# Five moves of work in a gated attention and expert layer: head sums, block turning, query copies, a shared multiply, and pool order

## The chip, the cores and the metric

The kernel runs on one core of a Trainium2 chip. The metric is the time of the whole program on the device in microseconds (us); the time before is the median of three runs. The engines of the core are named as in the profile: PE (matrix engine), DVE (vector engine), ACT (scalar engine), POOL (GpSimd) and SP (the engine that here issues most of the DMA transfers). Each takes its own instructions strictly in order, and waits for the others by semaphores.

## The reference

A layer with gates: cross attention to a short context, then a mixture of experts, both added to the input through a tanh gate.

```python
# x (4, 512, 512), ctx_512 (4, 64, 128), float32; 16 heads of 32; 8 experts, top 2, inner width 256
def attn(q, latent_kv, Wq, Wkv_expand, Wout):
    k, v = split(latent_kv @ Wkv_expand.T)           # 64 keys a batch
    scores = einsum('bhqd,bhkd->bhqk', heads(q @ Wq.T), heads(k)) / sqrt(32)
    scores = where(tril(ones((512, 64))), scores, finfo.min)
    return merge(softmax(scores) @ heads(v)) @ Wout.T

def ffn(x, gate_w, w1, w2, w3, ws1, ws2, ws3):
    weights, idx = top_k(softmax(x @ gate_w.T), 2)
    y = sum over the two chosen e of weights * (silu(x @ w1[e].T) * (x @ w3[e].T)) @ w2[e].T
    z = silu(x @ ws1.T) * (x @ ws3.T) @ ws2.T        # the shared expert
    return y + z

x = x + tanh(g_xattn[0]) * attn(layernorm(x), ctx_512, Wq, Wkv_expand, Wout)
x = x + tanh(g_ffn[0]) * ffn(layernorm(x), ...)
```

## The kernel before

**Stages.** Attention runs from 0 to 184 us, once for each batch `b` of 512 tokens (four tiles `t` of 128 tokens). `last_routing` (184 to about 230 us) finishes the last batch: its output projection, second layernorm, gate, and the scatter of rows to their experts, with the shared expert in between. Then 34 expert tiles of 128 rows follow (to 430 us), which fetch rows by expert, multiply by w1 and w3 (L947), by w2 (L974), and add into `y_d`. A tail joins the two experts of each token, the shared expert and the residual.

**Order.** Attention and `last_routing` are under a manual schedule of all five engines: the order of the instructions on each engine is the order in which the Python code issues them. A step of batch `b` carries pieces of three batches: the scores and softmax of `b`, the output projection and second layernorm of `b - 1` (called `last`), and the first layernorm, transposes and query projection of `b + 1` and `b + 2`.

**The step of one batch**, in the order of issue in `attention()`: the products of scores for tiles 0 and 1 (`score_products`, into `psc`, the one buffer of pool `ps_s`); `largest` (the mask is added for tile 0, L321, then the maximum, L322) and `exponentials` (difference on DVE, L327, exponential on ACT, L328) of tiles 0 and 1, which gives p0 and p1; then the output projection of `last` by tiles (`project_out`: PE L368 into `pd`, DVE adds to `xs`, L372) with `moments` of the result; the turning of blocks for `b + 1`; `deviation` (a square root on ACT, L162, then `table_of(AF.Exp)`, a second table load, L675); the second half of the scores; the query projection of `b + 1` by quarters (`project_q`: PE L290 into `pq`, ACT copies to `qt`, L294); p2 and p3; `transpose_p` of p0 and p1 (PE L343 into `pp`, ACT copies to `prt`, L346); and so on. `ps_mm`, which `pd`, `pq`, `pp`, `pt` and others share, has four buffers.

**How the rows of the first layernorm are transposed.** For b = 0 and 1, PE transposes them (`turn`, L195, copies on ACT, L196). For b = 2 and 3, `first_rows` calls `passed` (L501 to L512): DVE normalizes the rows, SP writes them to DRAM (`xn_d`, four transfers of 256 KB) and reads them back with blocks in other places (`xg`, four transfers of 256 KB, in pieces of 128 floats, each filling 32 partitions of `xg`). Then `turn_blocks` (L517, four stream transposes of 32x32 blocks on DVE) makes `xt`. `first_rows(2, ...)` is issued at the end of the step of b = 0, so its `turn_blocks` stands in the step of b = 1; that of b = 3 stands in the step of b = 2.

**The start.** `head_of` (L118) holds, by partition, which of two heads the partition belongs to: two reductions of the identity matrix on DVE. The keys `kt` are made from the product `pk` by two scaled copies on ACT (L689) and two on DVE (L696), both scaled with `head_of`.

**The end of routing.** `fill(n)` draws n matmuls of the shared expert from `shared_in_turn`; when it draws the last one of a pair, the silu on ACT (L640) and a multiply on DVE (L641) are issued. `fill_ends` computes the ends of the experts' regions and issues eight transfers of zeros, half on SP and half on ACT. `tile_table` (L580 to L617) is a chain of DVE operations that makes a table of the tiles: first row, expert and rank of each. SP reads `row_of`, PE reads `expert_of`.

**Memory pools of attention.** `aw`, `ab`, `a2` and `a4` are allocated in this order and released together; then `w13_all`, the experts' first weights, is laid over their place.

Of the kernel before, what the change touches and what calls it, by code (L numbers as in the profile page):

```python
# [13 lines left out]
F32 = mybir.dt.float32  # L14
# [5 lines left out]
P = 128  # L20
# [28 lines left out]
def gated_cross_attention_moe(  # L49
# [64 lines left out]
    nc.gpsimd.memset(taken[0], 0.0)  # L114

    head_of = const.tile([P, 2], F32, name="head_of")
    for j in range(2):
        nc.vector.tensor_reduce(  # L118
            head_of[:, j : j + 1],
            ident.rearrange("p (i j d) -> p j i d", i=2, j=2)[:, j, :, :], AX.XY, ALU.add,  # L120
        )

    mask = const.tile([P, 1, 1, SK], F32, name="mask")
    nc.gpsimd.memset(mask, 0.0)
# [85 lines left out]
    weights = ctx.enter_context(ExitStack())  # L210

    with ExitStack() as attn:
        aw = attn.enter_context(tc.tile_pool(name="aw", bufs=1))
        ab = attn.enter_context(tc.tile_pool(name="ab", bufs=1))
        a2 = attn.enter_context(tc.tile_pool(name="a2", bufs=2))
        a4 = attn.enter_context(tc.tile_pool(name="a4", bufs=4))

        scoring = attn.enter_context(ExitStack())
        ps_s = scoring.enter_context(tc.tile_pool(name="ps_s", bufs=1, space=PSUM))


        wkv_sb = aw.tile([L, 2 * D], F32, name="wkv_sb")
        wo_sb = al.tile([P, DC, D], F32, name="wo_sb")
        ctx_sb = aw.tile([L, B, 2, SK], F32, name="ctx_sb")
        for t in range(2):
            nc.sync.dma_start(out=xs[0][:, t, :], in_=x[ts(t, P), :])
        nc.sync.dma_start(out=ctx_sb[:, :, 0, :], in_=ctx_t)
# [46 lines left out]
        def project_values(b):  # L274

            pv = ps_mm.tile([P, NPAIR, 2, HD], F32, tag="mm", name="pv")
            nc.tensor.matmul(
                pv.rearrange("p n j d -> p (n j d)"),
                ctx_sb[:, b, :, :].rearrange("p r k -> p (r k)"),
                wkv_sb[:, D : 2 * D], start=True, stop=True,  # L280
            )
            for j in range(2):
                r = slice(j * SK, (j + 1) * SK)
                nc.scalar.copy(vals[r, b, :, :], pv[r, :, j, :])
# [40 lines left out]
        def exponentials(pr, by_row, src, mx):  # L325

            nc.vector.tensor_tensor(by_row, src, mx, ALU.subtract)  # L327
            nc.scalar.activation(pr, pr, AF.Exp, scale=1.0 / math.sqrt(HD))  # L328
            return pr
# [147 lines left out]
            return places, scatter  # L477

        def new_xt():
            return ab.tile([P, DC, S], F32, tag="xt", name="xt")  # L480

        def new_qt():
            return a2.tile([P, DC, S], F32, tag="qt", name="qt")
# [11 lines left out]
            return passed(xn, b) if b > 1 else xn  # L495

        def new_xn():
            xn = ab.tile([P, QT, D], F32, tag="xn", name="xn")
            return [xn[:, t, :] for t in range(QT)]

        def passed(xn, b):  # L501


            for t in range(QT):
                nc.sync.dma_start(out=xn_d[b][ts(t, P), :], in_=xn[t])
            xg = ab.tile([P, QT, QT, P], F32, tag="xn", name="xg")
            for a in range(DC):
                nc.sync.dma_start(
                    out=xg[ts(a, HD)].rearrange("k t tb n -> k (t tb) n"),
                    in_=xn_d[b][:, ts(a, P)].rearrange("(t k) n -> k t n", k=HD),  # L510
                )
            return xg  # L512

        def turn_blocks(xg, dst):

            for t in range(QT):
                nc.vector.transpose(  # L517
                    dst[:, :, ts(t, P)].rearrange("p c (tb k) -> p tb c k", k=HD),
                    xg[:, t].rearrange("p tb (c i) -> p tb c i", c=DC),
                )  # L520
# [147 lines left out]
        def attention():  # L668
# [4 lines left out]
            def table_of(function):  # L673

                nc.scalar.activation(small_one, ones[:, 0:1], function)  # L675


            pw = ps_mm.tile([P, P], F32, tag="mm", name="pw")
            for _ in range(10):
# [37 lines left out]
            for b in range(B):  # L717
                more, last = b + 1 < B, b - 1
                prt = ab.tile([P, NPAIR, S], F32, tag="prt", name="prt")
                psc = score_products(b, 0, qt)  # L720
                if b > 1:
                    places, scatter = route(last - 1, *chosen)
                if more:
                    xt, qt_next = new_xt(), new_qt()
                    if not b:
                        turn(xn, xt)
                if not b:
                    project_values(1)
                p0 = exponentials(*largest(psc, 0))
                p1 = exponentials(*largest(psc, 1))  # L730
                if not b:
                    nc.scalar.activation(tg_x, tg_x, AF.Tanh)
                    nc.scalar.activation(tg_f, tg_f, AF.Tanh)
                if b > 1:
                    places()
                softmax(p0)
                if b:
                    mv, rstd = new_stats()
                    project_out(last, at, 0)
                    moments(last, mv, 0)  # L740
                softmax(p1)
                if b > 1:
                    for t in range(QT):
                        scatter(t)
                if b:
                    for t in range(1, QT):
                        project_out(last, at, t)
                        moments(last, mv, t)
                        if more and t == 1:
                            turn_blocks(xn, xt)  # L750
                    rest = deviation(mv, rstd)
                    if more:
                        table_of(AF.Exp)
                else:
                    project_q(xt, qt_next, range(2))
                    first_rest = first_moments(b + 2)
                    table_of(AF.Exp)
                psc = score_products(b, 1, qt)
                if not b:
                    transpose_p(p0, prt, 0)  # L760
                    transpose_p(p1, prt, 1)
                if b and more:
                    project_q(xt, qt_next, range(1))
                elif b:
                    gated, _ = shared_pair(*next(parts))
                    table_of(AF.Exp)
                p2 = largest(psc, 2)
                if b:
                    rest()
                p2 = exponentials(*p2)  # L770
                p3 = largest(psc, 3)
                if more:
                    p3 = exponentials(*p3)
                if b:
                    if more:
                        project_q(xt, qt_next, range(1, 2))
                    else:
                        gated()
                    xn2 = new_rows(last)
                    second_rows_of(xn2, last, mv, rstd)  # L780
                softmax(p2)
                if more:
                    softmax(p3)
                if b:
                    transpose_p(p0, prt, 0)
                    transpose_p(p1, prt, 1)
                    if not more:
                        turn(xn2, x2t[last])
                if more:
                    project_q(xt, qt_next, range(2, 3))  # L790
                    if b:
                        turn(xn2, x2t[last])
                    if b + 2 < B:
                        if b:
                            first_rest = first_moments(b + 2)
                            table_of(AF.Exp)
                        xn = first_rows(b + 2, first_rest)
                    project_q(xt, qt_next, range(3, DC))
                    if b == B - 2:
                        load_shared()  # L800
                    if b:
                        scored = gate(last)
                else:
                    p3 = exponentials(*p3)
                    softmax(p3)
                    gated, scored = shared_pair(*next(parts), lambda: gate(last))
                    gated()
                    scores = by_token(scored)
                transpose_p(p2, prt, 2)
                if not b:  # L810
                    project_values(2)
                elif more:
                    scores = by_token(scored)
                transpose_p(p3, prt, 3)
                if not b:
                    project_values(3)
                attended = []

                def attend_now():
                    attended.append(attend(b, prt))  # L820

                if b:
                    chosen = (xn2, *choose(last, scores, attend_now))
                else:
                    attend_now()
                (at,) = attended
                qt = qt_next
# [7 lines left out]
        def last_routing(at, chosen, parts):  # L835
# [3 lines left out]
            def fill(n):  # L839
                for _ in range(n):  # L840
                    next(filling)
# [31 lines left out]
            fill_ends(n)  # L873
            for t in range(QT):
                scatter(t)
            table = tile_table(n)
            for _ in filling:
                pass
# [274 lines left out]
```

## Time and profile before

| what | value |
|---|---|
| median of the runs before | 465.02 us (464.71 to 465.4) |
| the profiled execution | 463.8 us |
| its span, first instruction to last | 462.1 us |
| mean granted clock of PE | 0.998 |
| PE busy | 445.0 us of the span |
| DVE busy | 257.3 us |
| POOL busy | 178.5 us |
| ACT busy | 125.1 us |
| longest wait of PE behind a copy of queries (b = 2) | 2.07 us |
| idle of DVE ahead of the mask add of b = 1 | 4.29 us |
| idle of ACT ahead of its first copy of keys | 2.25 us |

The busy time of an engine says how much work it has over the whole span; it does not say which engine sets the end of a stage. For that one reads, in the timeline, what an engine was idle for: the bracket behind an instruction gives the idle time just before it and the instruction that ended it. The profiled execution was 1.2 us shorter than the median of the runs, and the span leaves out another 1.7 us around the program.

### The profile page before, as it was taken

How to read it: one execution, taken by the hardware profiler on the slowest of the kernel's cores; microseconds unless marked ns; L12 is line 12 of the kernel's file. 1: busy time of each engine (PE TensorE's matmuls, PEld its weight loads, DVE VectorE, ACT ScalarE, POOL GpSimd, SP SyncE). 2: the span in 40 equal slices, each digit the busy share in tenths (PEclk: the TensorE clock that was granted, in tenths of full speed). 3: DMA queues.
4: the chain of work that ended last, by engine and by line, in shares of the span. 5: the costliest groups of instructions: out<-in, count | busy, mean ns of one | idle time of the engine just before them, and what ended most of it. 6: DMA issues, size and time to landing. Idle time of an engine off the chain costs nothing.

```text
span 462.1 us, 6310 instructions
## 1 busy us (share of the span) xinstructions
PE 445.0 (96%) x1754; PEld 228.0 (49%) x1754; DVE 257.3 (56%) x613; ACT 125.1 (27%) x237; POOL 178.5 (39%) x184
## 2 busy tenths in 40 slices
PE   6999999899899999999999999999999999999994
PEld 6875545564455554454444444444444444444342
DVE  5759699789928974548223333334433333432385
ACT  3357613652354275322101111111111111111000
POOL 2003312303840573332400656555655655565400
PEclk9999999999999999999999999999999999999999
DMA  8987250070403040999943877666656666544598
GB/s 270 315 292 279 91 92 0 1 177 6 176 22 84 23 165 1 357 417 417 403 110 84 166 125 123 107 97 100 93 93 102 103 103 97 78 48 51 78 383 315
DMA packets 60800, 69.86 MB, mean 151 GB/s; under 512 B 11984, under 2 KB 44496, under 8 KB 59600
## 3 DMA queue, kind: packets, MB, share of 16 engines
q1 hardware_dynamic: 47536, 50.68, 35.4%
q0 software_dynamic: 12352, 17.57, 21.2%
q10 hardware_dynamic: 864, 1.08, 0.6%
q8 instruction: 17, 0.28, 0.2%
q14 instruction: 31, 0.25, 0.2%
HBM read 36.94 MB, written 32.37 MB: 150 GB/s over the span
## 4 chain that ended last, share of the span: by engine, by line
PE 77%; DVE 17%; ACT 3%; issue 2%; DMA 1%; DVEq 0%; ACTq 0%
PE ph L947 25%; PE py L974 13%; PE pq L290 8%; PE pd L368 6%; PE ph L659 6%; PE ph L633 5%; PE pz L1008 3%; DVE pr L327 3%; DVE mx L322 2%; DVE st L153 2%; PE pt L195 2%; PE psc L304 2%; DVE yk L1078 2%; PE pg L966 2%; PE po L357 2%
## 5 line engine op out<-in xcount | busy, mean ns | idle before, releaser
L981 POOL DMA_INDIRECT y_d<-y,meta x68 | 105.6, 1553 | 102.3 <-DVE y L978 58.3
L947 PE MATMUL ph<-w_all,xgt 128*128 x272 | 122.5, 593 | 0.1
L336 POOL TENSOR_TENSOR pr<-pr,rs 128x1024 f32<-128x1024 f32 x16 | 30.2, 1900 | 114.9 <-DVE rs L335 114.9
L947 PEld LDWEIGHTS ph<-w_all,xgt 128*128 128x128 f32 x272 | 49.1, 190 | 49.6 <-issue 49.5
L974 PE MATMUL py<-w_all,gt 128*128 x136 | 63.9, 592 | 0.0
L958 DVE SCALAR_TENSOR_TENSOR g<-sl,w,ph 128x256 f32<-128x256 f32 x34 | 16.3, 481 | 83.5 <-ACT sl L956 83.5
L290 PE MATMUL pq<-xt,wq_sb 128*128 128x512 f32 (+1 forms) x160 | 57.5, 512 | 2.5 <-ACT xt L196 1.3
L368 PE MATMUL pd<-wo_sb,at 128*128 128x512 f32 x128 | 56.2, 596 | 0.0
L956 ACT ACTIVATE sl<-ph 128x256 f32<-128x256 f32 x34 | 13.0, 383 | 108.1 <-PE ph L947 56.8
L290 PEld LDWEIGHTS pq<-xt,wq_sb 128*128 128x128 f32 x160 | 29.6, 190 | 25.6 <-issue 19.1
L974 PEld LDWEIGHTS py<-w_all,gt 128*128 128x128 f32 x136 | 25.8, 190 | 32.5 <-issue 32.5
L978 DVE COPY y<-py 128x512 f32<-128x512 f32 x34 | 23.5, 691 | 27.8 <-PE py L974 27.8
L368 PEld LDWEIGHTS pd<-wo_sb,at 128*128 128x128 f32 x128 | 23.9, 190 | 29.2 <-issue 26.8
L1008 PE MATMUL pz<-sh,gs_sb 128*128 128x512 f32 (+1 forms) x68 | 28.1, 570 | 1.4 <-DVE y L978 0.9
L935 DVE STREAM_TRANSPOSE xgt<-xg 128x512 f32<-128x512 f32 x34 | 23.9, 702 | 8.8 <-DMA xg<-xg_d 8.8
L659 PE MATMUL ph<-x2t,sh 128*128 128x512 f32 x64 | 28.4, 595 | 0.0
L968 ACT COPY gt<-pg 128x256 f32<-128x256 f32 x34 | 12.7, 372 | 52.8 <-PE pg L966 52.8
L153 DVE BATCH_NORM_STATS2 st<-x 128x6 f32<-128x512 f32 x32 | 21.7, 679 | 5.5 <-DMA x<-in_x_dram 4.9
L328 ACT ACTIVATE pr<-pr 128x1024 f32<-128x1024 f32 x16 | 17.0, 1061 | 23.4 <-DVE pr L327 19.7
L1008 PEld LDWEIGHTS pz<-sh,gs_sb 128*128 128x128 f32 x68 | 12.7, 190 | 16.6 <-issue 15.1
L333 DVE TENSOR_REDUCE sm<-pr 128x16 f32<-128x1024 f32 x16 | 19.1, 1194 | 1.6 <-ACT pr L328 1.6
L343 PE MATMUL pp<-ident,pr 128*128 128x128 f32 x128 | 16.4, 275 | 3.6 <-ACT qt L294 3.6
(167 smaller groups left out, 482.9 us busy)
## 6 DMA issues: line engine op xcount, KB each, us to landing
xg<-xg_d SPq DMA_DIRECT2D x144, 64.0 KB
w_all<-in_w_dram SPq DMA_DIRECT2D x8, 1024.0 KB
y_d<-gs_sb SPq DMA_DIRECT2D x1, 4352.0 KB
w_all<-in_w_dram SPq DMA_DIRECT2D x8, 512.0 KB
yk<-y_d SPq DMA_DIRECT2D x8, 512.0 KB
out_dram<-yk SPq DMA_DIRECT2D x15, 256.0 KB
x<-in_x_dram SPq DMA_DIRECT2D x3, 1024.0 KB
xn_d<-xn SPq DMA_DIRECT2D x8, 256.0 KB
```

Of the source, the lines that this page charges most:

```text
L153: nc.vector.bn_stats(st, xs[b][:, t, :])
L290: nc.tensor.matmul(pq, wq_sb[:, k, ts(c, P)], xt[:, k, tokens], start=(k == 0), stop=(k == DC - 1),)
L336: nc.gpsimd.tensor_tensor(pr, pr, rs.broadcast_to([P, NH, SK]), ALU.mult)
L368: nc.tensor.matmul(pd, at[:, c, ts(t, P)], wo_sb[:, c, :], start=(c == 0), stop=(c == DC - 1),)
L633: nc.tensor.matmul(ph, sh13[:, w, k, ts(f, P)], x2t[b][:, k, :], start=(k == 0), stop=(k == DC - 1),)
L659: nc.tensor.matmul(ph[:, w, :], sh13[:, w, k, ts(f, P)], x2t[b][:, k, :], start=(k == 0), stop=(k == DC - 1),)
L935: nc.vector.transpose(xgt.rearrange("p c t k -> p t c k"), xg.rearrange("p t (c i) -> p t c i", c=DC))
L947: nc.tensor.matmul(ph, xgt[:, k, :], w13_all[:, ds(e, 1), :, k, :], start=(k == 0), stop=(k == DC - 1),)
L974: nc.tensor.matmul(py, gt[:, f, :], w2_all[:, ds(e, 1), f, :], start=(f == 0), stop=(f == FC - 1))
L978: nc.vector.tensor_copy(y, py)
L981: nc.gpsimd.indirect_dma_start(out=y_w[h], out_offset=IndirectOffsetOnAxis(ap=goes[j][:, h : h + 1].bitcast(I32), axis=0), in_=y[:, ts(h, ...
L1008: nc.tensor.matmul(pz, gs[b][:, f, ts(t, P)], sh2[:, f, columns], start=(f == 0), stop=(f == FC - 1),)
```

## The change

Five edits.

1. The two reductions of `head_of` are issued in `attention()`, where they come first in DVE's order; they stood behind the normalize of the first two tiles.
2. `turn_blocks` for b = 1 (which makes `xt` of batch 2) is issued ahead of `largest(psc, 0)`; it stood behind the second `project_out` and `moments`. For b = 2 it stays where it was.
3. For b = 1 and 2, the second quarter of the query projection, `project_q(xt, qt_next, range(1, 2))`, is issued ahead of `largest(psc, 3)` and the exponential of p3. PE's order does not change by this; ACT copies the queries ahead of that exponential instead of behind it.
4. `fill(3)` ahead of `tile_table(n)`: the last matmuls of the second pair of the shared expert, with silu and multiply, are issued ahead of the table. PE's and ACT's orders do not change; DVE multiplies ahead of the table.
5. A new pool `ae` comes first and takes `wkv_sb`, `ctx_sb`, `xt`, `xn` and `xg` from `aw` and `ab`, and `a2` moves to the second place.

The orders of PE, POOL and SP are the same before and after.

```diff
     head_of = const.tile([P, 2], F32, name="head_of")
-    for j in range(2):
-        nc.vector.tensor_reduce(
-            head_of[:, j : j + 1],
-            ident.rearrange("p (i j d) -> p j i d", i=2, j=2)[:, j, :, :], AX.XY, ALU.add,
-        )
...
     with ExitStack() as attn:
+
+        ae = attn.enter_context(tc.tile_pool(name="ae", bufs=1))
+        a2 = attn.enter_context(tc.tile_pool(name="a2", bufs=2))
         aw = attn.enter_context(tc.tile_pool(name="aw", bufs=1))
         ab = attn.enter_context(tc.tile_pool(name="ab", bufs=1))
-        a2 = attn.enter_context(tc.tile_pool(name="a2", bufs=2))
         a4 = attn.enter_context(tc.tile_pool(name="a4", bufs=4))
...
-        wkv_sb = aw.tile([L, 2 * D], F32, name="wkv_sb")
+        wkv_sb = ae.tile([L, 2 * D], F32, name="wkv_sb")
         wo_sb = al.tile([P, DC, D], F32, name="wo_sb")
-        ctx_sb = aw.tile([L, B, 2, SK], F32, name="ctx_sb")
+        ctx_sb = ae.tile([L, B, 2, SK], F32, name="ctx_sb")
...
-            return ab.tile([P, DC, S], F32, tag="xt", name="xt")
+            return ae.tile([P, DC, S], F32, tag="xt", name="xt")
...
-            xn = ab.tile([P, QT, D], F32, tag="xn", name="xn")
+            xn = ae.tile([P, QT, D], F32, tag="xn", name="xn")
...
-            xg = ab.tile([P, QT, QT, P], F32, tag="xn", name="xg")
+            xg = ae.tile([P, QT, QT, P], F32, tag="xn", name="xg")
...
                 nc.scalar.activation(small_one, ones[:, 0:1], function)
 
+            for j in range(2):
+                nc.vector.tensor_reduce(
+                    head_of[:, j : j + 1],
+                    ident.rearrange("p (i j d) -> p j i d", i=2, j=2)[:, j, :, :], AX.XY, ALU.add,
+                )
...
                 if not b:
                     project_values(1)
+                if b == 1:
+                    turn_blocks(xn, xt)
                 p0 = exponentials(*largest(psc, 0))
                 p1 = exponentials(*largest(psc, 1))
...
                         moments(last, mv, t)
-                        if more and t == 1:
+                        if b == 2 and t == 1:
                             turn_blocks(xn, xt)
...
                 p2 = exponentials(*p2)
+                if b and more:
+                    project_q(xt, qt_next, range(1, 2))
                 p3 = largest(psc, 3)
                 if more:
                     p3 = exponentials(*p3)
                 if b:
-                    if more:
-                        project_q(xt, qt_next, range(1, 2))
-                    else:
+                    if not more:
                         gated()
...
             for t in range(QT):
                 scatter(t)
+            fill(3)
             table = tile_table(n)
             for _ in filling:
                 pass
```

## The prediction

> **What bounds the kernel now.** I read the busy table and the chain of waits first. (±0.2% is about what a measurement of this kernel can tell from no change.)
>
> ```profile
> PE 445.0 (96%) x1754; PEld 228.0 (49%) x1754; DVE 257.3 (56%) x613; ACT 125.1 (27%) x237; POOL 178.5 (39%) x184
> ...
> PE 77%; DVE 17%; ACT 3%; issue 2%; DMA 1%; DVEq 0%; ACTq 0%
> ...
> L343 PE MATMUL pp<-ident,pr 128*128 128x128 f32 x128 | 16.4, 275 | 3.6 <-ACT qt L294 3.6
> ```
>
> The matrix engine is busy 96% and no expert tile is touched, so an edit can win only a gap of PE in front of 184 us, and can lose whatever makes a new gap. From 213.57 to 240.4 PE runs without a gap and then the tiles run at PE's pace: a shift of attention reaches the end one to one. The last row is the gap edit 3 aims at: two gaps, both behind the copy of second queries. The timelines of b=1, DVE first, then PE and ACT (columns: start, duration, engine, line, operation, count, idle before and its releaser):
>
> ```profile
> 51.95 1.92 DVE L182 TENSOR_SCALAR xn<-x,mv,rstd 128x512 f32<-128x512 f32 x4
> 58.16 1.23 DVE L321 TENSOR_TENSOR psc<-psc,mask 128x1024 f32<-128x1024 f32 x1 [4.29 <-PE psc L304]
> ...
> 70.27 2.49 DVE L517 STREAM_TRANSPOSE xt<-xg 128x512 f32<-128x512 f32 x4
> 72.69 0.71 DVE L372 SCALAR_TENSOR_TENSOR x<-pd,tg_x,x 128x512 f32<-128x512 f32 x1
> ```
> ```profile
> 71.97 2.06 PE L304 MATMUL psc<-kt,qt 64*128 64x128 f32 x32
> 73.95 7.13 PE L290 MATMUL pq<-xt,wq_sb 128*128 128x512 f32 x16
> 80.93 1.47 PE L343 MATMUL pp<-ident,pr 128*128 128x128 f32 x12
> 83.91 0.66 PE L343 MATMUL pp<-ident,pr 128*128 128x128 f32 x4 [1.51 <-ACT qt L294]
> 84.41 3.69 PE L290 MATMUL pq<-xt,wq_sb 128*128 128x512 f32 x8
> ```
> ```profile
> 82.33 1.06 ACT L328 ACTIVATE pr<-pr 128x1024 f32<-128x1024 f32 x1 [1.33 <-DVE pr L327]
> 83.29 0.57 ACT L294 COPY qt<-pq 128x512 f32<-128x512 f32 x1
> ```
>
> The 4.29 us ahead of 58.16 are the idle stretch. But the turn reads xg, which travels DVE→DRAM→SBUF after 53 us. The same stretch by windows (last columns: granted clock, DMA share, GB/s):
>
> ```profile
> 60.00:61.00 1.00, 1.00 (x4) 0.43 (x3) 0.96 (x2) 0.00 (x0) 0.00 (x0) 1.00 1.23 190
> ...
> 63.00:64.00 1.00, 1.00 (x4) 0.44 (x3) 0.96 (x2) 0.06 (x1) 0.00 (x0) 1.00 0.23 33
> 64.00:64.50 0.50, 0.50 (x2) 0.19 (x1) 0.50 (x2) 0.11 (x1) 0.00 (x0) 1.00 0.07 18
> 64.50:65.00 0.50, 0.50 (x2) 0.19 (x1) 0.50 (x1) 0.50 (x1) 0.00 (x0) 1.00 0.00 0
> ```
>
> The writes of xn_d move 53.2–56.2; the four reads are issued 56.73–58.64, move at 165–198 GB/s with every engine full, are mostly in by 63.3, and the last engine is done at 64.48. DVE is free at 53.87. Each of the four reads fills 32 partitions of xg, and each transpose reads all 128: already the first one needs the last read. So the data comes some 6.3 us after the mask add could start.
>
> **Edit 2, the turn ahead of the maxima (b=1).** DVE works in order, so everything queued behind the four transposes waits with them: mask add, maxima, exponent arguments of p0 and p1 (hence ACT's exponentials), sums, the residuals of t=0..3 and through them PE's buffers. The turn takes 2.49 us from 64.5: it ends at 67.0, and the mask add starts there instead of 58.16: +8.82. At 70.27 a turn of 2.49 drops out: from the residual of t=2 on, DVE is +6.36 (72.69 → 79.05).
> PE hides only a little:
> - Second half of the scores: needs the last read of psc (exponent argument of p1, 63.07+1.22+8.82 = 73.1), starts 73.2 instead of 71.97, to 75.3.
> - The first two quarters of pq, 16 matmuls, 7.1 us: 75.3 to 82.4. The residuals, though late, free its buffers in time (t=0 at 75.2).
> - Transposes of p0, 0.7 us: 82.4 to 83.2; then PE needs a buffer, which the first qt copy frees. That copy stands on ACT behind two table loads (sd: 76.20–77.70; exponential: 77.72–79.2). They follow the variance, +6.36: sd waits to 82.56, the copy is at 85.48–86.05.
> - Last transposes of p1 wait for the second qt copy. On ACT now: exponential of p2 86.3–87.36, copy 87.4–87.97 (edit 3), exponential of p3 88.69–89.75, first prt copy to 90.3.
> - The third quarter of the query projection (pq at 84.41 above) needs the buffer that this prt copy frees: it starts at 90.35: **+5.94**.
> From there PE keeps its order and the later copies have slack. POOL's products and the DVE moments behind are pushed by no more than 6.36, with the same releasers. The turn of b=2 stays where it was. Bounds: landing at 63.3 (mass in) gives +4.8; a tail that ends 0.5 later gives +6.4 (the last engine also served an instruction fetch, which can fall elsewhere).
>
> **Edit 3, copy before exponential of p3.** At b=2 the gap is 2.07 (125.57–127.64). The exponential runs 126.05–127.11, the copy 127.02, prt 127.48. Turned round: the copy ends at about 125.3, exponential (126.05–127.11) and the first prt copy behind it (to 127.65) then decide: the third quarter of pq starts at 127.7 instead of 128.13: **−0.43**. The gap isn't gone; the prt copy is late next. The exponential isn't delayed, as its own argument comes at 125.95. At b=1 its 0.46 is inside the +5.94. Bounds: 0 to −0.9.
>
> **Edit 1, head sums ahead.**
>
> ```profile
> 8.42 0.34 DVE L118 TENSOR_REDUCE head_of<-ident 128x1 f32<-128x64 f32 x2
> ...
> 8.73 1.26 ACT L689 ACTIVATE kt<-pk,head_of 128x512 f32<-128x512 f32 x2 [2.25 <-DVE head_of L118]
> 9.89 1.07 ACT L196 COPY xt<-pt 128x512 f32<-128x512 f32 x2
> 11.01 1.16 PEld L290 LDWEIGHTS pq<-xt,wq_sb 128*128 128x128 f32 x6 [1.55 <-ACT xt L196]
> ```
>
> DVE is idle to 4.31 and ident is there at 1.64, so the two reductions cost nothing in front. ACT's kt waits then for pk alone (first half done at about 7.85): 7.9–9.16. The xt copies need pt, whose first 4 transposes end near 9.2: 9.3–10.37. PE starts pq at 10.42 instead of 11.01: **−0.59**. Wq is in by 10.0. Bounds: 0 (x's later rows land at 10.9 and could set the pace of the second half) to −0.7.
>
> **Edit 4, second shared pair before the tile table.** The multiply (0.69, at 222.15, waiting for ACT's silu) now stands ahead of the table (215.21–220.84, 5.63 us): the table runs 222.84–228.47. Who waits: SP's first fetch, busy with end fills till 228.82; the experts' register at about 230; the ranks at 240; the fetch itself waits for the landing of xg_d at 234.95. **0**, with margins of 0.4 to 1.5 us. If the cover is gone, the first fetch moves with row_of, and I bound that at +2. ACT issues the same silu in the same place, so nothing is won either.
>
> **Edit 5, pools.** The first load of w13 still overlaps the prt tile in the new order (ae 22K, a2 16K, aw 12K, prt behind them at 50–66K of w13's first 64K), so its wait on the last copies of prt stands; its issue stays at 184.68 and the weights are hidden anyway. **0**; engine orders of PE, POOL and SP are as before.
>
> **Sum.** 5.94 − 0.43 − 0.59 = +4.92. The profiled execution: 463.8, span 462.1; so 468.7 and 467.0. The median of the runs is 465.02, 1.2 above the profiled one: **469.9** (+1.06%).
>
> **A rule against the row.** The page "DMA: Bandwidth & Descriptors" of the Trainium skill (Specifications) says that pieces of 512 bytes and more reach line rate. The reads of xg are of 512 bytes (2048 of them, 1.05 MB), and the row shows 165–198 GB/s at a full share. At the 373–389 GB/s which the trace shows for the writes of xn_d, they would be in at about 60.9: b=1 costs then +2.24, and the total is 466.2. I take the row. The same page (Rules for kernel authors) wants a wait on a transfer put late, with compute between; edit 2 does the reverse, and the compute which covered it (58.16–70.27) is now behind it.
>
> **Rivals.**
> 1. The transfer is in when DVE falls idle (reads that start sooner, say). Then the turn fits in the 4.29 and b=1 gains its gap, 1.41: −2.43, **462.6**, faster. It decides from a landing before 55.6 on; against it the reads are issued only at 56.73. 5%.
> 2. Landing near 60.9, as above: **466.2**. 5%.
> 3. As forecast, and the clock falls too. Between 83.2 and 90.35 PE does 8 transposes (0.9 us), with gaps up to 2.9 us. "TensorE: Matmul & The Clock Gate" (Why this matters for your kernels) wants no idle of PE over about 3 us, and has one idle window of some 3.4 us bring half rate. The row of before: stretches of 4.0–4.5 us of transposes and gaps (124.10–128.13, 167.46–171.98) kept 1.00, and at the end the clock falls 4.2 us after the last work (456.2, 0.71 in 460–461). So a thin 7 us could go either way: by the rows no drop, by the rule a stretch of 3.4–6.8 us at half rate, +1.7 to +3.4: **472.4**. 36%.
> 4. Edit 4 makes the first fetch late: +1 to +2, about 471.4. 4%.
> The forecast itself: 50%. Range 468.4–473.2: it leaves out cases 1 and 2. Faster 5%, same 3% (landing early and a larger gain at the start), slower 92%.
>
> **What would show it.** DVE's four transposes after an idle of some 6 us on xg ahead of them; the mask add at about 66.4 (66.98 less the start's 0.59); PE's first pq at 10.4; PE waiting on qt and prt copies between 82 and 90; the third quarter of pq of b=2 about 0.4 earlier against its batch's start; the tile table near 233, without a new wait for SP or PE; first tile near 245.2 instead of 240.26; a PEclk row below 1.00 near 87–95 or not. Wrong would make it: no idle ahead of the transposes, a landing much before 63, or PE finding other work between 83 and 90.

## The result and the profile after

The changed kernel takes 471.05 us (median of four runs, 470.4 to 471.22) against 465.1 us (464.71 to 465.4): a ratio of 1.0126, 95% interval 1.0108 to 1.0143. It is slower by 6 us. The profiled execution took 471.22 us, its span is 469.5 us, the mean granted clock 0.99 instead of 0.998. One later execution of the kernel before was slow (672.51 us at a mean clock of 0.657) and stands in no ratio and no count below.

The page of the kernel after: PE's busy time, the row of the granted clock in 40 slices, and the groups of query projections and of transposes of p.

```profile
PE 447.5 (95%) x1754; PEld 229.3 (49%) x1754; DVE 257.6 (55%) x613; ACT 125.0 (27%) x237; POOL 178.4 (38%) x184
...
PEclk9999999799999999999999999999999999999999
...
L287 PE MATMUL pq<-xt,wq_sb 128*128 128x512 f32 (+1 forms) x160 | 59.9, 529 | 5.2 <-ACT prt L343 4.2
...
L340 PE MATMUL pp<-ident,pr 128*128 128x128 f32 x128 | 16.5, 275 | 4.0 <-ACT qt L291 4.0
```

PE has as many instructions as before and is busy 2.5 us longer; 2.4 of that are in pq (57.5 before, 59.9 now). One slice of the clock is at 7 tenths, the one around 88 us. The idle time has grown: behind qt copies 4.0 instead of 3.6, and ahead of pq 5.2 instead of 2.5, of which 4.2 now lie behind prt copies.

The timeline of DVE in the step of b=1 (start, duration, engine, line, operation; in brackets the idle time before and its releaser):

```profile
51.44 1.91 DVE L177 TENSOR_SCALAR xn<-x,mv,rstd 128x512 f32<-128x512 f32 x4
64.59 2.49 DVE L514 STREAM_TRANSPOSE xt<-xg 128x512 f32<-128x512 f32 x4 [11.24 <-DMA xg<-xn_d]
67.00 1.20 DVE L318 TENSOR_TENSOR psc<-psc,mask 128x1024 f32<-128x1024 f32 x1
```

DVE's idle time there is 11.24 us where it was 4.29, and it ends with a transfer instead of with the scores. The mask add starts at 67.00 instead of 58.16. What PE makes of it:

```profile
82.21 1.04 PE L340 MATMUL pp<-ident,pr 128*128 128x128 f32 x8
86.17 0.63 PE L340 MATMUL pp<-ident,pr 128*128 128x128 f32 x4 [2.92 <-ACT qt L291]
87.85 0.72 PE L340 MATMUL pp<-ident,pr 128*128 128x128 f32 x4 [1.05 <-ACT qt L291]
90.24 6.11 PE L287 MATMUL pq<-xt,wq_sb 128*128 128x512 f32 x8 [1.67 <-ACT prt L343]
96.19 1.91 PE L190 MATMUL pt<-ident,xn 128*128 128x128 f32 x16
```

Before, the third quarter of pq started at 84.41 and took 3.69 us. Now it starts at 90.24 and takes 6.11. The windows around it show why (first number behind the length: busy time of PE; last three columns: granted clock, DMA share, GB/s):

```profile
84.00:88.00 4.00, 0.78 (x5) 0.57 (x6) 3.76 (x8) 3.52 (x6) 0.00 (x0) 1.00 0.00 0
88.00:92.00 4.00, 2.33 (x6) 1.10 (x6) 3.90 (x8) 2.99 (x5) 0.00 (x0) 0.54 0.00 0
92.00:96.00 4.00, 4.00 (x7) 1.68 (x6) 3.79 (x9) 0.00 (x0) 3.76 (x2) 0.61 0.00 0
96.00:100.00 4.00, 4.00 (x22) 2.70 (x21) 0.59 (x3) 3.59 (x6) 0.00 (x0) 1.00 0.01 4
```

PE worked 0.78 of the four microseconds from 84 to 88; then the clock is at half, from 88.31 to 95.13 by the trace's record of the granted clock.

The sum of the difference of the two profiled executions, from the starts of the same PE instructions:

| where | us |
|---|---|
| first pq, 11.01 to 10.49 | −0.52 |
| third quarter of pq of b=1, 84.41 to 90.24, less the line above | +6.35 |
| the eight matmuls of that quarter, in part at half clock, 3.69 to 6.11 | +2.42 |
| third quarter of pq of b=2, 128.13 to 135.90, less the lines above | −0.48 |
| transposes of second rows in b=3: a pause of ACT before, none after | −1.12 |
| tail: additions in the last stage and the last stores | +0.75 |
| span, 462.1 to 469.5 | +7.40 |

The line of b=3 does not follow the edits, as the profiles of the experiments show. Nor do the edits make the difference between the 7.40 here and the 5.95 of the medians: the profiled execution of before was one of its shorter ones (463.8 against a median of 465.1), that of after an ordinary one (471.22 against 471.05).

### The profile page after: what moved, and what is told of

It reads as the page before. It is cut to its first block, busy times and chain, and to the rows that moved or that the text cites. A ratio compares the mean times of both kernels' runs of the same rounds, so it can differ in the third digit from the quotient of the medians.

```text
span 469.5 us, 6308 instructions
## 1 busy us (share of the span) xinstructions
PE 447.5 (95%) x1754; PEld 229.3 (49%) x1754; DVE 257.6 (55%) x613; ACT 125.0 (27%) x237; POOL 178.4 (38%) x184
## 4 chain that ended last, share of the span: by engine, by line
PE 67%; DVE 17%; DMA 9%; ACT 2%; issue 1%; SPq 1%; DVEq 0%; ACTq 0%
PE ph L952 23%; PE py L979 11%; PE pq L287 7%; PE pd L365 6%; PE ph L656 6%; DMA y_d<-y,meta 5%; PE ph L630 4%; DVE pr L324 3%; DVE mx L319 3%; DVE sm L330 2%; PE pt L190 2%; DVE st L148 2%; DMA yk<-y_d 2%; PE early L630 1%; PE pg L971 1%; DMA xg<-xn_d 1%
## 5 line engine op out<-in xcount | busy, mean ns | idle before, releaser
L287 PE MATMUL pq<-xt,wq_sb 128*128 128x512 f32 (+1 forms) x160 | 59.9, 529 | 5.2 <-ACT prt L343 4.2
L979 PE MATMUL py<-w_all,gt 128*128 x136 | 63.9, 593 | 0.0
L287 PEld LDWEIGHTS pq<-xt,wq_sb 128*128 128x128 f32 x160 | 30.6, 196 | 30.2 <-issue 20.3
```

What stands on the lines that cost most here:

```text
L287: nc.tensor.matmul(pq, wq_sb[:, k, ts(c, P)], xt[:, k, tokens], start=(k == 0), stop=(k == DC - 1),)
L979: nc.tensor.matmul(py, gt[:, f, :], w2_all[:, ds(e, 1), f, :], start=(f == 0), stop=(f == FC - 1))
```

## The experiments

Each was timed beside the kernel before on the same chip. The medians of the kernel before were 465.73, 464.37 and 465.96 us in the three groups of four, so ratios are compared, and positions in the traces.

**All but the turn.** The change without edit 2.

```diff
-                if b == 1:
-                    turn_blocks(xn, xt)
...
-                        if b == 2 and t == 1:
+                        if more and t == 1:
                             turn_blocks(xn, xt)
```

> The kernel after, with the turning of blocks back where it stood (edits 1, 3, 4 and 5 stay). Theory (the turn's wait and the clock drop behind it are the whole loss): the start's 0.52 and edit 3's 0.46 and 0.48 remain as gains, 465.1 - 1.5 = 463.6 us, granted clock 1.00 throughout attention, PE's third quarter of pq in b=1 near 83.4. Rival (edits 4 or 5 take some of it, or a later stage absorbs the gain): 464.8 or more.

Measured: 463.85 us, ratio 0.996 (0.9944 to 0.9975). Third quarter of pq in b=1 at 83.56, clock 1.00 throughout attention. The whole loss, and more, goes with edit 2; the rest of the change gains.

**The turn alone.** The kernel before with edit 2.

> The kernel before with the early turn alone. Theory: DVE waits for xg till about 65.1 (the reads start 0.5 later than in the kernel after), PE's third quarter of pq goes from 84.41 to about 91.3 (+6.9: the copy of queries now stands behind the exponential of p3), then some 6.8 us at half clock cost 2.4: 465.1 + 9.3 = 474.4 us; 473.3 if the 0.9 us wait of ACT at 170 is gone as it is in the kernel after. Rival (the clock falls only with edit 3's order, or the wait is shorter without edit 1): 472.0 or less.

Measured: 473.14 us, ratio 1.0173 (1.0156 to 1.019). PE in b=1:

```profile
90.63 1.12 PE L343 MATMUL pp<-ident,pr 128*128 128x128 f32 x4 [3.45 <-ACT qt L294]
91.53 5.50 PE L290 MATMUL pq<-xt,wq_sb 128*128 128x512 f32 x8
```

The third quarter starts at 91.53, where 91.3 was expected, and is slow again: the clock falls without edit 3 as well (half from 88.53 to 95.35). So edit 2 does it by itself. The span is 9.8 us over that of the first profile of before, near the 9.3 of the theory; the medians are only 7.4 apart. Part of the difference is the clock of the kernel before, taken up below under edit 3: its 27 executions on this chip with a mean clock of 0.996 or more have a median of 465.07, 8.1 below. The remaining 1.7 us are not explained.

**PE kept at work.** The kernel after, with ten matmuls added between PE's transposes of b=1.

```diff
+                for _ in range(extra[half]):
+                    nc.tensor.matmul(pp.rearrange("p i n -> p (i n)"), ident, flat[:, 0:512],
+                                     start=True, stop=True)
...
-                    transpose_p(p0, prt, 0)
-                    transpose_p(p1, prt, 1)
+                    transpose_p(p0, prt, 0, (3, 3) if b == 1 else (0, 0))
+                    transpose_p(p1, prt, 1, (2, 2) if b == 1 else (0, 0))
```

> The kernel after, with ten matmuls of 128x512 added on PE in its thin stretch of b=1 (3 ahead of each half of the transposes of p0, 2 ahead of each half of p1; what they write is overwritten). Nothing else moves: the waits on the copies stay. Theory (the half clock from 88.3 to 95.2 is a consequence of the thin stretch and costs 2.4): granted clock 1.00 through 82-98, the third quarter of pq back at 3.7 us for 8 matmuls, 471.05 - 2.4 = 468.6 us, and no more than 0.4 lost to the added work. Rival (the clock falls for another reason, or the eight matmuls were slow from waiting on data): clock still below 1.00, 471 us or, with the added work in the way, 471.5.

Measured: 472.18 us, ratio 1.0152 (1.0135 to 1.0169), so the expected time was missed. The clock stayed at 1.00, but each added matmul became two PE instructions and took 0.87 us, twice what the edit reckoned with, and the third quarter of pq started only at 92.60. Second rows follow at 96.04, against 96.19 with the half clock: the added work ate what the clock gave. It was repeated with less:

**Five matmuls**, (1, 2) and (1, 1) in the same edit.

> The kernel after with five matmuls of 128x512 added on PE in the thin stretch of b=1 (1 and 2 ahead of the halves of p0's transposes, 1 and 1 ahead of p1's), instead of the ten that took 0.87 us each and held the third quarter of pq to 92.6. Theory (the half clock costs 2.4 and comes from the thin stretch): third quarter of pq still at 90.2, its eight records in 3.7 us, clock 1.00 from 84 to 98, PE's transposes of second rows at 93.8 instead of 96.2; about 2.4 less than the kernel after, that is a ratio near 1.0075 to the kernel before. Rival (the added work takes as much as the clock gave): ratio 1.0126.

Measured: 470.21 us, ratio 1.0103 (1.0076 to 1.013). The windows:

```profile
84.00:88.00 4.00, 3.51 (x15) 1.77 (x14) 3.80 (x8) 3.49 (x5) 0.00 (x0) 1.00 0.00 0
88.00:92.00 4.00, 3.17 (x10) 1.47 (x10) 3.90 (x8) 2.99 (x5) 0.00 (x1) 1.00 0.00 0
```

The waits are where they were, ACT's and DVE's columns differ by less than 0.1 from those of the kernel after, the third quarter of pq starts at 90.20 and takes 3.70, second rows are at 93.74: 2.45 us earlier. In the traces that shows the cause and the size of the clock's share: more work on PE in the thin stretch, the same waits, the full clock. All six timed executions had a mean clock of 0.996 or more, those of the kernel after 0.991 or less. The times alone do not show it: the interval of the ratio begins just above the expected 1.0075 and reaches past the rival's 1.0126.

**One matmul**, (0, 0) and (1, 0).

> The kernel after with a single matmul of 128x512 added, ahead of the first half of p1's transposes (it starts near 86.2, inside the clock's window 84.9 to 88.3, which held 1.1 us of transposes and no matmul). Theory (a window falls when it holds almost no matmul work): 0.86 us of matmul keeps the clock at 1.00 and the time goes as with five matmuls, ratio near 1.0075. Rival (a window needs about half its length of work, or of matmuls): half clock from 88.3 to 95.1, ratio near 1.0126.

Measured: 470.4 us, ratio 1.009 (1.0065 to 1.0115). In the profiled execution the clock fell again (half from 89.10 to 95.93), although PE worked 1.25 us between 85.69 and 89.10, most of it on the added matmul. In five of its seven timed executions the mean clock was 0.994 or less, in two it was 0.996. The rival holds for the profile: one matmul isn't enough. In other executions it may have been, if 0.996 means no drop. The last section says on what that depends.

**The turn behind the exponent argument of p1.**

```diff
-                if b == 1:
-                    turn_blocks(xn, xt)
                 p0 = exponentials(*largest(psc, 0))
                 p1 = exponentials(*largest(psc, 1))
+                if b == 1:
+                    turn_blocks(xn, xt)
```

> The kernel after, with the turn of b=1 issued behind the exponent argument of p1 (about 64 us) instead of ahead of the mask add. Theory (what costs is DVE waiting for xg; 2.49 us of turning alone are covered): DVE's wait shrinks to 0.7 us or less, the scores start at 57.6 as before, the residuals of t=0 and 1 come some 3 us later, which PE's four buffers cover; the third quarter of pq within 0.5 of the kernel with the old place: 463.6 to 464.2 us, clock 1.00. Rival (any turn ahead of the residuals holds PE through its buffers): 466 us or more.

Measured: 464.28 us, ratio 0.9983 (0.9967 to 0.9998).

```profile
62.61 1.22 DVE L324 TENSOR_TENSOR pr<-psc,mx 128x1024 f32<-128x1024 f32 x1
64.41 2.49 DVE L514 STREAM_TRANSPOSE xt<-xg 128x512 f32<-128x512 f32 x4 [0.58 <-DMA xg<-xn_d]
```

The wait shrinks to 0.58, and the third quarter of pq comes at 84.01, 0.45 later than with the turn in its old place. An earlier turn is no loss as such; the loss is what DVE cannot do while it waits.

**Reading whole rows.** The kernel after, with xg read in pieces of 2 KB.

```diff
-                    out=xg[ts(a, HD)].rearrange("k t tb n -> k (t tb) n"),
-                    in_=xn_d[b][:, ts(a, P)].rearrange("(t k) n -> k t n", k=HD),
+                    out=xg[ts(a, HD)].rearrange("k t tb n -> k t (tb n)"),
+                    in_=xn_d[b].rearrange("(t k) n -> k t n", k=P)[ts(a, HD)],
```

> The kernel after, with xg read back from DRAM in pieces of 2 KB (whole rows) instead of 512 bytes; the regrouping of blocks is left out, so batches 2 and 3 attend to other rows than the reference's. Theory (the small pieces set the 5 us of the reads): xg complete near 61.0 instead of 64.6, the mask add near 63.4, PE's third quarter of pq near 86.7; 471.05 - 3.6 = 467.5 us with the half clock, 465.1 without. Rival (the rate is set by reading back DRAM just written, or by the queue, whatever the pieces): landing near 64.6 and about the time of the kernel after.

Measured: 470.02 us, ratio 1.0112 (1.0079 to 1.0145).

```profile
63.85 2.49 DVE L514 STREAM_TRANSPOSE xt<-xg 128x512 f32<-128x512 f32 x4 [10.61 <-DMA xg<-xn_d]
```

DVE goes on 0.74 earlier than in the kernel after, 0.11 of it from an earlier start. Pieces four times as long bought some 0.6 us instead of 3.6. The theory that the small pieces set the 5 us falls. What does was not separated: reading back what was just written, the four transfers themselves, or that each read fills only 32 of the 128 partitions, in both runs, while each write empties all 128.

**Edit 1 alone.**

> The kernel before with edit 1 alone. Theory: PE's first pq at 10.5 instead of 11.0 and the whole rest shifted by it: 0.5 us faster than the kernel before on this chip. Rival (the gain at the start is taken back by a later wait of PE, as on wq or x): no difference.

Measured: 464.12 us, ratio 0.999 (0.997 to 1.001): not told apart from no difference by its time. In the trace the first pq starts at 10.88; on the same chip it starts at 11.17 and 11.18 in the two kernels without edit 1, and at 10.38 in the other one with it. So it gains 0.3 to 0.8 there, 0.5 between the first two profiles. In a later profile with edits 1 and 3, PE starts there at 10.59, having waited for the landing of wq_sb: that is late next.

This profile also holds what nobody had asked for. PE in b=2, where this kernel is the same as before, and a window there:

```profile
123.98 1.47 PE L338 MATMUL pp<-ident,pr 128*128 128x128 f32 x12
127.52 0.66 PE L338 MATMUL pp<-ident,pr 128*128 128x128 f32 x4 [2.07 <-ACT qt L289]
128.01 5.39 PE L285 MATMUL pq<-xt,wq_sb 128*128 128x512 f32 x8
```
```profile
128.00:132.00 4.00, 4.00 (x8) 1.70 (x7) 2.37 (x4) 1.41 (x3) 2.68 (x2) 0.57 0.00 0
```

The gap of 2.07 behind the copy of queries brings half clock in this execution, from 128.39 for 3.41 us, and the eight matmuls take 5.39 instead of 3.69. In the first profile of before the same gap went without it.

**Edit 3 alone.**

> The kernel before with edit 3 alone. Theory: PE's third quarter of pq 0.46 earlier in b=1 and another 0.48 in b=2, 0.9 us faster than the kernel before on this chip, less up to 0.6 where ACT's stop among the prt copies near 170 us grows from 0.9 to 1.7 as it did in the kernel with edits 1, 3, 4 and 5. Rival (the copy only exchanges its wait with the exponential): no difference.

Measured: 461.84 us, ratio 0.995 (0.9926 to 0.9974): 2.3 us, more than twice what was expected. In the trace the third quarter of pq of b=2 starts at 127.31; on the same chip, with the same start (11.17 and 11.18), it starts at 128.30 without edit 3. That is 1.0, near the expected 0.9 for b=1 and 2 together. The rest goes with the clock. Over the three groups, 39 of 92 timed executions of the kernel before had a mean clock under 0.996; within a group their median was 1.3 to 2.5 us longer. Of the 66 executions of the five kernels with edit 3 and without the turn ahead of the mask add, one had. Two traces (this chip's kernels without edit 3) show where: b=2, as above. That all the 39 fell there is inferred. It fits that against those 18 executions of the kernel before on this chip that had 0.996 or more (median 462.98) edit 3 gains only 1.1 us.

**Edits 4 and 5 alone.**

> The kernel before with edits 4 and 5 alone. Theory: same time as before within 0.2%, w13's first issue near 184.7, the tile table 6 to 8 us later, SP's first fetch where it was (near 235), PE's first tile near 240.3. Rival (the late table holds the first fetch): SP's fetch and the first tile later by 1 us or more, and the time with it.

Measured: 464.98 us, ratio 1.0003 (0.9983 to 1.0023). PE is 0.74 later than in the first profile of before ahead of the table, and so is everything that could have slipped: w13's first issue at 185.42 (184.68 before), SP's first fetch at 235.67 (234.95), the first tile at 241.00 (240.26). No part of the change.

**Edits 1 and 3 alone.**

> The kernel before with edits 1 and 3 alone. Theory (the gains of the change are these two, 4 and 5 are nothing): the gain of edit 3 alone (ratio 0.995) and 0.5 us of the start: ratio 0.994, the same as with edits 1, 3, 4 and 5 (0.996) within the measurement. Rival (4 or 5 carry some of it): 0.997 or more.

Measured: 462.57 us, ratio 0.9943 (0.9922 to 0.9963), as expected.

**A further step.** With edits 1 and 3, the transposes and copies of p0 also ahead of the exponential of p3.

```diff
                 if b and more:
                     project_q(xt, qt_next, range(1, 2))
+                    transpose_p(p0, prt, 0)
...
                 if b:
-                    transpose_p(p0, prt, 0)
+                    if not more:
+                        transpose_p(p0, prt, 0)
                     transpose_p(p1, prt, 1)
```

> The kernel before with edits 1 and 3, and the transposes and prt copies of p0 also issued ahead of the exponential of p3 (b=1 and 2; PE's order stays). Theory (what is late next behind edit 3 is the first prt copy, which stands behind that exponential): PE's gap ahead of the third quarter of pq goes from 1.07 to about 0.1 in b=1 and from 1.63 to about 0.1 in b=2, together 2.4 us less than with edits 1 and 3 alone, ratio near 0.989. Rival (the exponential of p3, now about 0.5 us later in b=2, becomes late for the softmax and the transposes of p3): no more than 1 us, ratio 0.992 or more.

Measured: 459.09 us, ratio 0.9866 (0.9843 to 0.9889): 6 us faster than the kernel before and faster than the change. PE, then ACT, in b=1:

```profile
80.26 1.91 PE L338 MATMUL pp<-ident,pr 128*128 128x128 f32 x16
82.00 3.60 PE L285 MATMUL pq<-xt,wq_sb 128*128 128x512 f32 x8
```
```profile
80.95 1.07 ACT L341 COPY prt<-pp 128x512 f32<-128x512 f32 x2
81.91 1.07 ACT L323 ACTIVATE pr<-pr 128x1024 f32<-128x1024 f32 x1
```

No bracket is left on PE: both gaps are closed, and those of b=2 too (third quarter at 123.34 instead of 126.69 with edits 1 and 3 alone). These 3.35 us, of which 0.2 are an earlier start, are more than the 2.4 expected; where the rest comes from was not followed up. The exponential of p3 starts at 81.91; its argument is there at 81.56 (80.34 and 1.22 on DVE), so it loses some 0.35 us, and no wait of PE behind it is seen in b=1 or 2.

## Why the prediction was right, and where it was wrong

**Direction and mechanism** were right: +4.92 was forecast, on the wait of the turn for xg, and +5.95 is what the medians show. Removing the early turn turns the loss into a gain, and adding it to the kernel before makes the loss.

**The size of edit 2's wait** was 0.4 to 0.6 short. The forecast had DVE go on at the end of the last packet (64.48, or 63.9 with the earlier start). The last packet of xg ends at 63.88 in the kernel after, as it should; DVE starts at 64.59, 0.7 later. The same 0.7 is there with the turn behind p1 (63.74 to 64.41) and with whole rows (63.16 to 63.85). The term that was left out is the time from the last packet to the waiting engine's start. Behind it every step of the walk through ACT and PE was in its place: third quarter of pq forecast at 89.8 with the earlier start, found at 90.24.

**The clock** was the wrong choice. “By the rows no drop” was given the larger chance and set the predicted time; the rival with the drop (+1.7 to +3.4) is what happened, with 6.83 us at half clock and +2.42. The step that failed is the comparison with the rows. The stretches of before that kept the clock were 4.0 and 4.5 us long, and PE worked 1.93 us of the window from 124 to 128 and more in the other. The forecast stretch had 0.9 us of work in 7.15. Nothing so thin stood in the rows of before, except at its end, where the clock did fall. Besides, one profile of before was taken for a proof that 124 to 128 keeps the clock; in two profiles of kernels with that same stretch it did not. The rule of the Trainium skill, page “TensorE: Matmul & The Clock Gate” (Why this matters for your kernels), pointed the right way, but its figure of about 3 us does not fit here: the longest gap was 2.92 us, and with edit 1 alone one of 2.07 was enough. With the drop the rival forecast 472.4 us; the range held 471.05.

**Edits 1, 3, 4, 5** were right in the traces: −0.52 for −0.59, −0.48 for −0.43 at b=2, and nothing for 4 and 5. The bound of −0.9 for edit 3 at b=2 left out a gain that the one trace of before could not show, the clock's.

**Rule against row for the transfer.** The row was rightly preferred to the rule of line rate from 512 bytes on (the Trainium skill, “DMA: Bandwidth & Descriptors”, Specifications). The theory put up afterwards, that small pieces are to blame, was wrong as well: 2 KB pieces land 0.6 earlier, not 3.6.

**Luck.** That the number came within 1.1 us is in part luck, as errors of opposite sign met: the drop raised the time by 2.42, and the kernel before is, in the median, 1.3 us longer than the profile on which the sum was made. The forecast added the whole difference to the median. Drops of the clock that edit 3 removes may be part of this 1.3; the clocks of those four executions are not on record.

## What to carry to other kernels

An idle stretch of an in-order engine is no place for work whose data is still under way: ask when the last byte lands, add the time to the waiting engine's start (0.7 us here), and count everything queued behind. A copy that frees a buffer PE needs goes ahead of a long operation that nobody waits for: here that order alone was worth more than anything else in the change. Where a matrix engine runs thin for a few microseconds, add up its work in each 3.4 us (the steps of the clock, below) instead of looking at the longest gap alone, and read the granted clock in several executions.

## What the runs showed of the hardware

**The clock falls on a grid.** The shortest drop, with edit 1 alone, lasts 3.413 us. In the first profile of before the full clock lasts from 6.44 to 460.41 us, which is 133 times that. In the kernel after it lasts 24 such steps, then 2 at half, then 109 at full. The grid's start differs between executions (4.85 to 10.59 us for the first rise here), so the same gap can fall within one step or be shared by two.

**What counts is the work of PE in one step, transposes included.** Three steps, in this order: in the kernel after ahead of its drop, with edit 1 alone ahead of its drop, and with the further step in b=3, where PE does nothing but transposes and the clock stays.

```profile
84.89:88.31 3.42, 1.09 (x8) 0.84 (x8) 3.39 (x4) 2.65 (x5) 0.00 (x0) 1.00 0.00 0
124.98:128.39 3.41, 1.34 (x10) 0.95 (x9) 3.41 (x6) 2.46 (x5) 2.64 (x9) 1.00 0.40 159
163.46:166.88 3.42, 2.69 (x25) 2.45 (x24) 3.32 (x8) 2.46 (x6) 2.50 (x10) 1.00 0.41 161
```

The fourteen profiles hold 1862 steps at full clock. Behind 20 of them the clock fell, at the end of the kernel or in attention; in these PE was busy 1.35 us or less. In the other 1842 it was busy 1.46 us or more. Matmuls alone do not sort them: steps without any matmul but with 2.06 to 2.69 us of transposes kept the clock. So the bound lies, in these runs, near 1.4 us of work in a step of 3.41. This is also where chance comes in for b=2 of the kernel before: in its first profile the thin stretch is shared by two steps with 3.08 and 1.68 us of work, and nothing falls; with edit 1 alone, and with edits 4 and 5 alone, one step holds only about 1.35.

**A pause of ACT.** In b=3 the prt copies of ACT stop for a moment, and PE with them. PE in the kernel before, then in the kernel after:

```profile
171.49 0.66 PE L195 MATMUL pt<-ident,xn 128*128 128x128 f32 x4 [0.81 <-ACT prt L346]
```
```profile
176.99 1.91 PE L190 MATMUL pt<-ident,xn 128*128 128x128 f32 x16
```

Of the fourteen profiles nine have PE's gap, of 0.73 to 1.39 us, at this very place, and five have none: the kernel after, edit 1 alone, edit 3 alone, edits 4 and 5 alone, and whole rows. It doesn't follow the edits. The last four of these were timed on one chip in one group; all eight of the other two groups have the gap. So among the experiments it goes with the chip or the hour rather than with the program. Its cause stays open.
